# 24 columns a step on VectorE, loads of 16 and 8 registers, one-hot rows of two groups at once, 180 tiles copied

## The chip, the cores and the metric

The kernel runs on one core of a Trainium2 chip. The core has a matrix engine (PE, TensorE), a vector engine (DVE, VectorE), a scalar engine (ACT, ScalarE), GpSimd (POOL) and SyncE (SP), each with its own stream of instructions, and 16 DMA engines. The metric is the device time of one execution in microseconds (us), as a median over several runs. A profile of one execution gives the span of its instructions and the records that are quoted here.

## The reference

One layer of a graph network on 12,500 nodes of 64 numbers and 212,500 edges of 32, sorted by destination, with a residual and a layer norm:

```python
msg_in = concatenate([nodes[row], nodes[col], edge_features], axis=-1)
messages = relu(msg_in @ mW1 + mb1) @ mW2 + mb2
aggregated = segment_sum(messages, col, num_segments=12500)
update = relu(concatenate([nodes, aggregated]) @ uW1 + ub1) @ uW2 + ub2
x = layernorm(nodes + update)
```

`row` is an edge's source and `col` its destination.

## The kernel before

**Tiling.** The edges lie in order of destination. A tile is 128 edges, a group is three tiles (`TG` = 3, `GE` = 384 edges), and there are `G` = 554 groups. As the edges are sorted, the destinations of a group lie in a window of `W` = 32 nodes, whose first node is read on the chip.

**A step.** The main loop (L560) has one step k for each group. PE runs three parts of three groups, one behind another (L574): `turn(k)`, which transposes the group's gathered rows and its one-hot rows; `hidden(k - 2)`, the first matmul of the message network; and `sums(k - 4)`, which adds the hidden rows into the window by a matmul with the one-hot rows. ScalarE copies the transposed rows out of PSUM (L351) and applies the relu (L377). VectorE adds the sums into `agg` and the edge counts into a row of `xc` (L406, L407), at an address that is read into a register. PE starts a step when what it needs of the steps before is there: the gather, the one-hot rows, ScalarE's copies, and the PSUM tiles (two sets, `own.ps[g % 2]`).

**One-hot rows.** `onehot(g)` (L326) compares each edge's place in the window with 0 to 31 and writes 128 x 3 x 32 numbers next to the gathered rows, in the ring `own.s` of eight buffers (`RING`). It is issued at the end of step k for group k + 2 (L588).

**Two ways to the source nodes.** A group's source rows come by indirect DMA from GpSimd, one for each tile (L149), issued four groups ahead (`AHEAD`). A gather waits until the transposes of the group that had the buffer before are done. For some groups (`COPIED`, L81), the first tile is not gathered: its 128 columns are copied from `xc`, which holds all nodes' features transposed on the chip, straight to the place where the transposed rows would go. `fetch(k)` (L475) does this in each step from 18 on: VectorE copies `VCOLS` = (8, 12) columns and ScalarE `ACOLS` = (12, 8). Each count stands for one load of so many registers (L490) with the addresses of the source columns, and then so many copies of a column of 64 numbers (L503 on VectorE, L505 on ScalarE). With 40 columns a step, 164 tiles are copied, and 1497 are gathered.

**Every fourth step** has more: `places` reads four windows' addresses into registers (L301, a load of 4) and copies the four windows of `xc` (L308); `windows` multiplies them on PE (L315), and VectorE copies the four results to `wm` (L320). When 512 nodes have all their edges, an update of them is spread over three steps (`update`, L413: L424 to L458), 25 times in all. The indices of the next columns are scaled by VectorE every eighth step (L473).

**Order.** The order on each engine is that of the program. On VectorE a step is: the update's part if there is one, the two adds, the four copies to `wm` in every fourth step, the one-hot rows, the index scaling if due, a load of 8 and 8 copies, a load of 12 and 12 copies, and in every fourth step a load of 4 with four window copies.

Of the kernel before, what the change touches and what calls it, by code (L numbers as in the profile page):

```python
# [15 lines left out]
ALU = mybir.AluOpType  # L16
# [4 lines left out]
P = 128  # L21
N = 12500
E = 212500
D = 64
# [5 lines left out]
W = 32  # L30
TG = 3
GE = TG * P
G = (E + GE - 1) // GE
SB = 4
AHEAD = 4
RING = AHEAD + 4
BLOCKS = 3
NW = 2 * SB
NH = 3
# [7 lines left out]
TIMES = 4  # L47
BEGIN = 18
CHECKED = 8
VCOLS = (8, 12)  # L50
ACOLS = (12, 8)
COLS = sum(VCOLS + ACOLS)
SPAN = 8


def tiles_of(g):

    n = min(GE, E - g * GE)
    return [min(P, n - j * P) for j in range((n + P - 1) // P)]


def plan():
# [4 lines left out]
    def least(g):  # L67
        q = min(1.0, g * GE / E)
        return g * GE * N / E - 6.0 * math.sqrt((E - N) * q * (1 - q)) * N / E - 6

    chunks, b = [], 0
    for e in [c * CH for c in range(1, N // CH + 1)] + [N]:
        n = e - b
        chunks.append((b, *((P, n // P) if n % P == 0 else (n // 2, 2)),
                       next((g for g in range(G) if least(g) >= e), G)))
        b = e
# [4 lines left out]
COPIED = []  # L81
while BEGIN - (-P * (len(COPIED) + 1) // COLS) < G - SHORT:
    COPIED.append(BEGIN - (-P * (len(COPIED) + 1) // COLS))


class Own:
# [4 lines left out]
    def __init__(self, nc, ctx):  # L91
        def on(name, *shape, of=nc.sbuf_tensor):
            return ctx.enter_context(of(name, list(shape), F32)).ap()

        self.s = [on(f"own_s{i}", P, TG, D + W) for i in range(RING)]
        self.st = [on(f"own_st{i}", P, SB * GE) for i in range(BLOCKS)]
        self.wm = [on(f"own_wm{i}", P, H) for i in range(NW)]
        self.h = [on(f"own_h{i}", P, TG, H) for i in range(NH)]
        self.ident = on("own_ident", P, P)
        self.one = on("own_one", P, 1)  # L100
        self.at = (nc.sbuf_base + 31) // 32 * 32
        self.xc = on("own_xc", P, NP)

        self.ps = [[on(f"own_ps{i}{k}", P, 512, of=nc.psum_tensor) for k in range(3)]
                   for i in range(2)]
# [3 lines left out]
def ordered(ctx: ExitStack, tc: tile.TileContext, a, own, ok):  # L109
# [3 lines left out]
    nc = tc.nc  # L113
# [17 lines left out]
    loads, places_by, copy_by, relu_by, sums_by, wm_by, turn_by = ({} for _ in range(7))  # L131
# [3 lines left out]
    def after(first, *others):  # L135

        tc.declare_no_dep(first.ins, group="quiet", reason="waits for the last of a step")
        for i in others:
            tc.add_manual_dep(
                first.ins, i.ins.name,  # L140
                mybir.DependencyInfo(mybir.DependencyClass.Sync, mybir.DependencyReason.DATA),
                reason="the kernel's own rings",
            )
        return first
# [31 lines left out]
    iota = iop.tile([P, W], F32, name="iota")  # L176
# [3 lines left out]
    nc.vector.memset(xc[:, N:], 0.0)  # L180
    first_i = temp.tile([P, G], I32, name="first_i")
    nc.sync.dma_start(first_i, a["firsts"].to_broadcast([P, G]))
    dlc_i = temp.tile([P, G * TG], I32, name="dlc_i")
    nc.sync.dma_start(dlc_i, a["dst_cols"])
# [13 lines left out]
    def bit(k):  # L198

        nodes = [NEAR_NODES + (N - NEAR_NODES) * i // BITS for i in (k, k + 1)]  # L200
        tiles = [first + (NT - first) * i // BITS for i in (k, k + 1)]
        nc.sync.dma_start(src_sb[:, slice(*tiles)], a["src"][:, slice(*tiles)])
        nc.sync.dma_start(xc[:D, slice(*nodes)], a["xT"][:, slice(*nodes)])


    halves = [(0, G // 2), (G // 2, G)]
    firsts_f = [own.ps[0][k][:, : g1 - g0] for k, (g0, g1) in enumerate(halves)]
# [12 lines left out]
    dlc = const.tile([P, G * TG], F32, name="dlc")  # L220
# [30 lines left out]
    def combined():  # L251

        wps = ups.tile([H, CH], F32, name="u_ps").rearrange("p (n h) -> p n h", n=4)
        nc.tensor.matmul(wps[:, 0], w2t, u1s, start=True, stop=True)
        nc.tensor.matmul(wps[0:1, 1], b2, u1s, start=True, stop=True)
        nc.vector.tensor_copy(wc, wps[:, 0])
        nc.vector.tensor_copy(ux[D : D + 1, :], wps[0:1, 1])
# [27 lines left out]
    def inputs(b):  # L285
        if b * SB >= G:
            return
        c0, c1 = b * SB * GE, min(E, (b + 1) * SB * GE)
        efs_by[b] = nc.sync.dma_start(own.st[b % BLOCKS][D + W :, : c1 - c0], a["efT"][:, c0:c1])
        after(efs_by[b], *([hidden_by[(b - BLOCKS + 1) * SB - 1]] if b >= BLOCKS else []))  # L290

    def columns(g):
        t, c = own.st[g // SB % BLOCKS], (g % SB) * GE
        return t, c, sum(tiles_of(g))

    def places(b):

        g, n = b * SB, min(SB, G - b * SB)
        if n <= 0:
            return  # L300
        _, v = nc.values_load_multi_w_load_instructions(  # L301
            start_i[0:1, g : g + n], engines=[ET.DVE], min_val=0, max_val=N - 1,
            skip_runtime_bounds_check_because="they were clamped to the nodes on the chip",
        )
        xw = xwp.tile([D + 2, SB, W], F32, name="xw")
        for i in range(n):
            starts[g + i] = v[i]
            nc.vector.tensor_copy(xw[:, i, :], xc[:, bass.ds(v[i], W)])  # L308
        xws[b] = xw, n
# [16 lines left out]
    def onehot(g):  # L326
        if g >= G:
            return
        places_by[g] = nc.vector.tensor_tensor(  # L329
            own.s[g % RING][:, :, D:], iota.unsqueeze(1).to_broadcast([P, TG, W]),  # L330
            dlc[:, g * TG : (g + 1) * TG].unsqueeze(2).to_broadcast([P, TG, W]), ALU.is_equal,
        )
        after(places_by[g], *([sums_by[g - RING]] if g >= RING else []))

    def turn(g, ps):

# [132 lines left out]
    def addresses(i):  # L469

        if i in indices:
            t = indices[i][:, : min(SPAN * COLS, P * len(COPIED) - i * SPAN * COLS)]
            nc.vector.tensor_scalar(t, t, 4.0, float(own.at), ALU.mult, ALU.add)  # L473

    def fetch(k):  # L475
# [8 lines left out]
        c0 = (k - BEGIN) * COLS  # L484
        for engine, count in [*((ET.DVE, c) for c in VCOLS), *((ET.Activation, c) for c in ACOLS)]:
            count = min(count, P * len(COPIED) - c0)
# [37 lines left out]
    def step(*work):  # L524


        parts, used = [], []
        for part, g in work:
            ps, old = own.ps[g % 2], users[part][g % 2]
            parts.append((part, g, *part(g, ps)))  # L530
            used += old
        did = [i for p in parts for i in p[2]]
        after(did[0], *used, *(i for p in parts for i in p[3]))
        copies = None
        for part, g, *_ in parts:
            if part is sums:
                for b in [b for b in xws if (b - 1) * SB <= g][:1]:
                    last, copies = windows(b, own.ps[g % 2][2][:, (TIMES + 1) * W :][:, :H])
                    did.append(last)
        for i in did[:-1]:  # L540
            tc.no_tile_sem_insts.add(i.ins.name)
            tc.add_to_no_dep_group("quiet", i.ins)
        for part, g, _, _, follow in parts:
            if part is sums:
                step_update(g)
            users[part][g % 2] = follow(did[-1])
            if part is sums and copies:
                copies()
                users[part][g % 2] += [wm_by[b * SB + i] for i in range(min(SB, G - b * SB))]

    inputs(0)
    inputs(1)
    onehot(0)
    onehot(1)
    places(0)
    windows(0, ups.tile([H, CH], F32, name="u_ps")[:, :H], False)[1]()
    indexes(0)
# [2 lines left out]
    for k in range(G):  # L560
        if k < BITS:
            bit(k)
        if k == CHECKED:
            addresses(0)
            combined()
            ordered_edges()
            early.close()
            up = ctx.enter_context(tc.tile_pool(name="upd", bufs=2))
        if k % SB == 2:
            inputs(k // SB + 2)  # L570
        if k % SB == 1:
            places(k // SB + 1)
        if k < G - SHORT:
            step((turn, k), *([(hidden, k - 2)] if k > 1 else []),  # L574
                 *([(sums, k - 4)] if k > 3 else []))
            made, summed = max(0, k - 1), max(0, k - 3)
        else:

            step((turn, k))
            for _ in range(2):  # L580
                if summed < made:
                    step((sums, summed))
                    summed += 1
            for _ in range(2):
                if made <= k:
                    step((hidden, made))
                    made += 1
        onehot(k + 2)  # L588
        fetch(k)
        if k + AHEAD < G:  # L590
            gather(k + AHEAD)
# [333 lines left out]
```

## Time and profile before

| | us |
|---|---|
| median of 3 runs | 1896.92 |
| lowest and highest | 1896.71, 1897.36 |
| the profiled execution | 1895.77 |
| span of its instructions | 1894.0 |

| engine | busy us | share of the span |
|---|---|---|
| PE | 1362.3 | 72% |
| VectorE | 1490.7 | 79% |
| ScalarE | 1555.3 | 82% |
| GpSimd | 1417.9 | 75% |

The granted clock of TensorE was 0.969. In the profile's groups a line stands as: source line, engine, operation, what it writes and reads, how often; then busy time in us and the mean of one in ns; then the idle time of the engine just before these instructions, and what ended it. "issue" means that the profile shows nothing that the engine waited for. DVEq and ACTq are the engines' instruction streams: loads of registers stand there and are not counted as busy. In a timeline a line has its start and length in us, and merged instructions carry a count.

### The profile page before, as it was taken

How to read it: one execution, taken by the hardware profiler on the slowest of the kernel's cores; microseconds unless marked ns; L12 is line 12 of the kernel's file. 1: busy time of each engine (PE TensorE's matmuls, PEld its weight loads, DVE VectorE, ACT ScalarE, POOL GpSimd, SP SyncE). 2: the span in 40 equal slices, each digit the busy share in tenths (PEclk: the TensorE clock that was granted, in tenths of full speed). 3: DMA queues.
4: the chain of work that ended last, by engine and by line, in shares of the span. 5: the costliest groups of instructions: out<-in, count | busy, mean ns of one | idle time of the engine just before them, and what ended most of it. 6: DMA issues, size and time to landing. Idle time of an engine off the chain costs nothing. (4 is left out here: it accounts for less than half of the span.)

```text
span 1894.0 us, 58313 instructions
## 1 busy us (share of the span) xinstructions
PE 1362.3 (72%) x12209; PEld 1194.1 (63%) x12209; DVE 1490.7 (79%) x13761; ACT 1555.3 (82%) x11818; POOL 1417.9 (75%) x1504
## 2 busy tenths in 40 slices
PE   3776777767767777677776776876767778767777
PEld 3666666666666666666665665766656667666665
DVE  3578888778888788887888878888888888887883
ACT  3489889888898888887988888889888888898882
POOL 7777777777777777777777777777777777777774
PEclk9999999999999999999999999999999999999999
DMA  5322222222222222222222222222222222222221
GB/s 136 73 46 45 46 48 44 51 44 47 46 45 48 46 43 51 45 47 43 48 51 43 48 46 45 46 48 44 51 44 48 46 47 45 47 44 50 47 44 29
DMA packets 68443, 92.52 MB, mean 49 GB/s; under 512 B 30893, under 2 KB 38350, under 8 KB 68078
## 3 DMA queue, kind: packets, MB, share of 16 engines
q0 software_dynamic: 47904, 49.12, 14.7%
q1 hardware_dynamic: 19260, 39.12, 7.2%
q14 instruction: 263, 2.15, 0.4%
q8 instruction: 102, 1.67, 0.4%
q10 hardware_dynamic: 914, 0.46, 0.1%
HBM read 85.29 MB, written 3.20 MB: 47 GB/s over the span
## 5 line engine op out<-in xcount | busy, mean ns | idle before, releaser
L149 POOL DMA_INDIRECT own_s<-in_x,src_sb x1497 | 1417.1, 947 | 457.4 <-issue 336.2
L503 DVE COPY own_st<-own_xc 64x4 uint8 x10500 | 895.3, 189 | 233.9 <-issue 221.5
L505 ACT ACTIVATE own_st<-own_xc 64x4 uint8 x10492 | 1058.0, 194 | 18.5 <-issue 15.4
L341 PE MATMUL own_ps<-own_ident,own_s 128*96 128x128 f32 x1661 | 289.1, 285 | 497.5 <-DMA own_s<-in_x,src_sb 149.2
L341 PEld LDWEIGHTS own_ps<-own_ident,own_s 128*96 128x96 f32 x1661 | 169.0, 132 | 567.8 <-ACT own_h L377 261.3
L394 PE MATMUL own_ps<-own_s,own_h 128*128 128x128 f32 x3322 | 481.3, 283 | 3.5 <-ACT own_h L377 3.0
L366 PE MATMUL own_ps<-own_wm,own_st 128*128 128x128 f32 x3322 | 478.8, 282 | 0.0
L351 ACT ACTIVATE own_st<-own_ps 96x384 f32<-96x384 f32 (+2 forms) x718 | 294.0, 410 | 203.8 <-PE own_ps L399 105.3
L394 PEld LDWEIGHTS own_ps<-own_s,own_h 128*128 128x128 f32 x3322 | 434.0, 199 | 5.1 <-ACT own_h L377 4.1
L366 PEld LDWEIGHTS own_ps<-own_wm,own_st 128*128 128x128 f32 x3322 | 431.0, 198 | 1.4 <-issue 0.5
L377 ACT ACTIVATE own_h<-own_ps 128x384 f32<-128x384 f32 x553 | 264.0, 477 | 15.0 <-PE own_ps L366 15.0
L399 PE MATMUL own_ps<-own_s,own_one 128*1 128x32 f32 x3322 | 190.2, 194 | 0.0
L320 DVE COPY own_wm<-own_ps 32x128 f32<-32x128 f32 x550 | 156.9, 285 | 5.6
L399 PEld LDWEIGHTS own_ps<-own_s,own_one 128*1 128x1 f32 x3322 | 114.6, 84 | 69.8 <-issue 6.7
L406 DVE TENSOR_TENSOR agg<-own_ps,agg 128x32 f32 x554 | 105.5, 190 | 64.3 <-PE own_ps L399 27.7
L329 DVE TENSOR_TENSOR own_s<-iota,dlc 128x96 f32<-128x96 f32 x554 | 142.5, 258 | 14.3 <-issue 0.2
L407 DVE TENSOR_TENSOR own_xc<-own_ps,own_xc 1x32 f32 x554 | 101.1, 183 | 29.3 <-PE u_ps L425 10.1
L308 DVE COPY xw<-own_xc 66x32 f32 x554 | 72.5, 214 | 15.3 <-DMA own_xc<-in_xT 9.2
L315 PE MATMUL own_ps<-w1b,xw 66*128 66x128 f32 (+1 forms) x276 | 69.1, 333 | 0.0
L446 ACT ACTIVATE rstd<-mv,eps 128x4 f32<-128x4 f32 (+1 forms) x25 | 7.4, 297 | 55.7 <-DVE mv L444 55.7
L437 PE MATMUL u_ps<-u,u 128*128 128x64 f32 (+1 forms) x196 | 50.3, 400 | 0.5 <-ACT u L427 0.5
L437 PEld LDWEIGHTS u_ps<-u,u 128*128 128x128 f32 (+1 forms) x196 | 47.2, 325 | 2.2 <-ACT u L427 0.9
(62 smaller groups left out, 278.0 us busy)
## 6 DMA issues: line engine op xcount, KB each, us to landing
own_st<-in_efT SPq DMA_DIRECT2D x138, 192.0 KB
own_s<-in_x,src_sb POOLq DMA_INDIRECT x1497
xin<-in_x SPq DMA_DIRECT2D x24, 128.0 KB
out<-o SPq DMA_DIRECT2D x24, 128.0 KB
own_xc<-in_xT SPq DMA_DIRECT2D x12, 179.2 KB
index<-in_src_copied SPq DMA_DIRECT2D x65, 1.2 KB
dlc_i<-in_dst_cols SPq DMA_DIRECT2D x1, 831.0 KB
own_xc<-in_xT SPq DMA_DIRECT2D x4, 179.5 KB
```

The costliest lines, as they stand in the source:

```text
L149: nc.gpsimd.indirect_dma_start(out=s[:p, j, :D], out_offset=None, in_=x[:, :], in_offset=bass.IndirectOffsetOnAxis(ap=src_sb[:p, g * TG + ...
L320: c = nc.vector.tensor_copy(wm[g % NW][D : D + W, :], wp[i * W : (i + 1) * W, :])
L329: places_by[g] = nc.vector.tensor_tensor(own.s[g % RING][:, :, D:], iota.unsqueeze(1).to_broadcast([P, TG, W]), dlc[:, g * TG : (g + 1) * ...
L341: nc.tensor.transpose(xt[:, j * P : j * P + p], s[:p, j, :], ident[:p, :p])
L351: after(nc.scalar.activation(t[r, c : c + n][:, m], xt[r, m], AF.Copy), step)
L366: nc.tensor.matmul(pre[:p, j, :], t[:, c + j * P : c + j * P + p], wm[g % NW], start=True, stop=True)
L377: relu_by[g] = [nc.scalar.activation(h, pre, AF.Relu)]
L394: did.append(nc.tensor.matmul(sg, h[:p, j, :], s[:p, j, D:].unsqueeze(1).to_broadcast([p, TIMES, W]), start=j == 0, stop=j == len(sizes) - 1))
L399: did.append(nc.tensor.matmul(counted, own.one[:p], s[:p, j, D:], start=j == 0, stop=j == len(sizes) - 1))
L406: after(nc.vector.tensor_tensor(agg[:, at], sg[:, 0, :], agg[:, at], ALU.add), step),
L503: by[engine] = nc.vector.tensor_copy(o, x_at)
L505: by[engine] = nc.scalar.activation(o, x_at, AF.Copy)
```

## The change

Three things are changed. VectorE copies 24 columns a step in place of 20, after a load of 16 registers and then one of 8, in place of 8 and then 12. The number of columns a step becomes 44, so that the formula at L81 gives 180 copied tiles in place of 164. The one-hot rows of two groups are written by one operation, issued in even steps alone, for which the ring's buffers are made in pairs. ScalarE's columns stay at 20 a step.

```diff
-VCOLS = (8, 12)
+VCOLS = (16, 8)
 ACOLS = (12, 8)
...
-        self.s = [on(f"own_s{i}", P, TG, D + W) for i in range(RING)]
+        self.two = [on(f"own_s{i}", P, 2 * TG, D + W) for i in range(RING // 2)]
+        self.s = [t[:, h * TG : (h + 1) * TG] for t in self.two for h in (0, 1)]
...
-        places_by[g] = nc.vector.tensor_tensor(
-            own.s[g % RING][:, :, D:], iota.unsqueeze(1).to_broadcast([P, TG, W]),
-            dlc[:, g * TG : (g + 1) * TG].unsqueeze(2).to_broadcast([P, TG, W]), ALU.is_equal,
+        places_by[g] = places_by[g + 1] = nc.vector.tensor_tensor(
+            own.two[g % RING // 2][:, :, D:], iota.unsqueeze(1).to_broadcast([P, 2 * TG, W]),
+            dlc[:, g * TG : (g + 2) * TG].unsqueeze(2).to_broadcast([P, 2 * TG, W]),
+            ALU.is_equal,
         )
-        after(places_by[g], *([sums_by[g - RING]] if g >= RING else []))
+        after(places_by[g], *([sums_by[g + h - RING] for h in (0, 1)] if g >= RING else []))
...
     onehot(0)
-    onehot(1)
...
-        onehot(k + 2)
+        if k % 2 == 0:
+            onehot(k + 2)
```

A group of 128 columns now ends every 2.9 steps in place of every 3.2, and the columns change hands between VectorE and ScalarE at other places.

More of the change, by code (lines that the diff above doesn't have):

```diff
@@ L33 @@
 G = (E + GE - 1) // GE
+assert G % 2 == 0
 SB = 4
```

## The prediction

> **What bounds the kernel now.** I read the busy totals first, then the idle columns of the costliest groups, then the timeline of one engine at a time.
>
> ```profile
> L149 POOL DMA_INDIRECT own_s<-in_x,src_sb x1497 | 1417.1, 947 | 457.4 <-issue 336.2
> L503 DVE COPY own_st<-own_xc 64x4 uint8 x10500 | 895.3, 189 | 233.9 <-issue 221.5
> ...
> 200.00:1800.00 1600.00, 1162.23 (x10490) 1020.37 (x10490) 1308.63 (x12276) 1374.44 (x10664) 1210.11 (x1280) 0.97 0.22 46
> ```
>
> The last line gives PE, weight loads, VectorE, ScalarE and GpSimd in turn. GpSimd looks only 75% busy, but 1280 gathers in 1600 us are one every 1.250 us, and the longest idle time before a gather in the table of waits is 1.4 us, once (0.3 otherwise): 0.947 of work and 0.30 of issue, without a pause. So the 1497 gathers make 1497 x 1.250 = 1871 us of the 1894, and 23 us lie at the ends. A step with copied columns (there are 525) issues 3 x 525 - 164 = 1411 gathers, 1764 us: 3.36 us a step. That is the bound. VectorE's column copies have 221.5 us of idle time that nothing explains but "issue". What that is shows in VectorE's own timeline, with the registers' loads beside it:
>
> ```profile
> 1006.55 0.19 DVE L406 TENSOR_TENSOR agg<-own_ps,agg 128x32 f32 x1
> ...
> 1009.50 0.17 DVE L406 TENSOR_TENSOR agg<-own_ps,agg 128x32 f32 x1
> 1009.70 0.18 DVE L407 TENSOR_TENSOR own_xc<-own_ps,own_xc 1x32 f32 x1
> 1009.92 0.26 DVE L329 TENSOR_TENSOR own_s<-iota,dlc 128x96 f32<-128x96 f32 x1
> 1010.44 0.67 DVE L503 COPY own_st<-own_xc 64x4 uint8 x8 [0.27 <-issue]
> 1011.61 1.21 DVE L503 COPY own_st<-own_xc 64x4 uint8 x12 [0.50 <-issue]
> 1012.49 0.33 DVE L406 TENSOR_TENSOR agg<-own_ps,agg 128x32 f32 x1
> ...
> 1015.13 0.20 DVE L406 TENSOR_TENSOR agg<-own_ps,agg 128x32 f32 x1
> ...
> 1019.03 0.19 DVE L406 TENSOR_TENSOR agg<-own_ps,agg 128x32 f32 x1
> ```
>
> ```profile
> L490 DVEq TENSOR_LOAD <-index x10: 593/720/845, 1004.2 to 1019.3; - x10
> ...
> L301 DVEq TENSOR_LOAD <-start_i x139: 339/344/596, 11.8 to 1863.6; - x139
> ```
>
> The second fence is the view of one source line: least, median and longest duration in ns. Ten loads at L490 split into those of 8 registers (0.595) and of 12 (0.845); L301 loads 4 (0.344). That is 62.6 ns a register and 94 ns besides. The engine's instruction stream hands nothing on while it loads, so the engine drains what it holds and then stands: the 0.27 and 0.50 us above. In the single records a step's stream is a strict chain: load of 8 (0.595), 0.322 to hand over 8 copies, load of 12 (0.845), 0.45 for 12 copies, 0.42 for the adds' register operations and the one-hot: 2.63, which is the step from 1012.49 to 1015.13 (2.64). A copy costs the engine 0.071 us (8 starts in a row), but the stream only (0.45 - 0.322)/4 = 0.032. The other ordinary steps (2.95, 2.99) hold a further pause of some 0.35 us, about once in four steps. The fourth, 1015.13 to 1019.03, has the four window copies (L320) and the next window reads (L308), whose 1.18 us of engine work cover both loads: 3.90. Four steps: 12.48, or 3.12 a step. All 525 average 3.36, so 0.24 a step (126 us) is the node updates and VectorE's waits for others; the waits are 94 us of it (the rows of agg, y and own_xc, from 27.7 down to 10.1). VectorE thus keeps up with GpSimd by a small margin only, though the page says 79% busy.
>
> **The change part by part.** Sums are against the profiled span of 1894.0 us; the runs' median, 1896.92, is 2.9 above it.
>
> *Gathers.* 180 tiles copied in place of 164 remove 16 gathers: 16 x 1.250 = 20 us off GpSimd's chain, giving 1874. Per column step GpSimd then needs (3 x 525 - 180) x 1.250 / 525 = 3.32 us. Whatever else takes over 3.32 a step decides.
>
> *Loads of 16 and 8.* No row has a load of 16. By the line through 4, 8 and 12 it is 94 + 16 x 62.6 = 1.095 us; below it can't sensibly be under the 12's 0.845, above two loads of 8 (1.19) bound it. I take 1.095. With 0.595 for the 8 that is 1.69 a step against 1.44: +0.25.
>
> One page speaks strongly against loading more registers. The Trainium skill, Runtime: NRT & Kernel Launch, Instruction fetch mechanics, puts a TENSOR_LOAD at about 200 ns a register; by it four more would cost 0.8 us a step and the sum would be some 420 us longer. The rows here show 62.6 ns, and 20 registers at 200 ns would not have fitted in the 3.36 us step of today.
>
> *Four more copies.* In the stream 4 x 0.032 = +0.13; on the engine 4 x 0.071 = +0.28, where the engine is the limit.
>
> *One-hot of two groups.* One operation in place of two takes about 0.03 from the stream every second step: -0.02. On the engine it is 128x192, which the trace does not have. Between 0.26 (as now) and 0.52 (twice) I take 0.36: from 32 elements at 0.190 (L406) to 96 at 0.258 an element costs 1.06 ns. It falls on the window steps (each has one), so there +0.10; the step without one loses 0.26 us of cover under the load of 16. It waits for the sums of two groups, the later one five steps back, long done.
>
> *An ordinary step* is bound by the stream: +0.25 + 0.13 - 0.02 = +0.36, so 3.00 plus pauses. Nothing covers it: a load of 1.095 has at most the add of own_xc and the one-hot (0.2 to 0.6 us) before it, so VectorE stands 0.5 to 0.9 us ahead of each 16 copies. Three of them: +1.08. From agg to agg 0.19 comes off once in four steps: the engine ends a step trailing its stream by the last copies, and 8 leave a lag of 0.33 where 12 left 0.52.
>
> *A window step* is bound by the engine: +0.28 (copies) +0.10 (one-hot) +0.18 (the load of 4 for L308 now stands behind 8 copies, 0.57 us, and no longer hides) -0.16 (the gap between the two groups of copies goes): +0.40.
>
> *Sum.* Four steps: 12.48 + 1.08 - 0.19 + 0.40 = 13.77, 3.44 a step, already over GpSimd's 3.32. The updates' own share stays (126 - 94 = 32 us, 0.06 a step; most of their 88 us of VectorE work lies in load gaps). Of the 94 us of waits, 0.18 a step, I keep 0.04: when VectorE is last, PE's results mostly lie ready; the bounds are 0 and 0.18. So 3.54 a step. 525 x (3.54 - 3.36) = +95 us: a span of 1989, with 2.9 around it **1992**.
>
> What is late next: PE's transposes (L341) need the one-hot and the PSUM that the adds (L406, L407) free, so PE, then ScalarE, then the freeing of own_s by the transposes are all paced by VectorE, and GpSimd starts to pause. ScalarE's 20 columns are as they were; the 16 split copies of L351 add some 0.18 us each, off the path.
>
> **The rivals.**
>
> A. *VectorE stays within GpSimd's pace*, so that the gain stands: 1874 + 3 = 1877, faster. It needs a step under 3.32, that is, 0.22 less than my sum. For it: a load of 16 at 0.845 (-0.25 in three of four steps, -0.19) and no waits (-0.04) would just do. Against it: three sizes of load lie on one line, and the chain 2.63 matches a measured step to 0.01.
>
> B. *The load gaps keep their size* and only engine work counts: the 16 copies cover the load of 8, which pays for the longer first load. Then a step is 2.75 busy (1308.63 x 3.36/1600), +0.28 copies, -0.08 one-hots, +0.42 gaps (221.5/525) = 3.37: 525 x 0.01 = 5 us, 1902. For it: window steps do hide loads. Against it: in the ordinary steps the stream, not the engine, sets 2.64.
>
> C. *VectorE's waits do not shrink*: all 0.18 remains, as updates are a round trip over PE and ScalarE (the sqrt of L446 waits 55.7 us for VectorE). 3.44 + 0.06 + 0.18 = 3.68: +168, 2065.
>
> **How the numbers follow.** Forecast 0.70, A 0.07, B 0.10, C 0.13. About 0.2% is what this kernel's measurement can tell from no change (1893 to 1901). Faster: A and a little of B, 0.09; same: part of B, 0.04; slower 0.87. Around the forecast the unknowns are the load (-99 to +37 us over 525 steps, three of four), the wide one-hot (-13 to +21, one in four) and the waits (-21 to +74). The range runs from 1922, short of B, to 2075, over C: A and B, 0.17, lie outside it.
>
> **What would show it.** Right: 1481 gathers at the same 947 ns but spaced wider than 1.25 us, with idle time now put down to PE or the transposes; VectorE's loads at L490 (L493 in the new file) near 595 and 1095 ns in equal numbers; "issue" idle before its copies up from 221.5 to about 300 us; agg to agg near 3.0 in ordinary and 4.3 in window steps; PE waiting for VectorE's lines. Wrong: gathers still every 1.25 us (A or B), a load of 16 well under 1.0 us, or VectorE's waits for PE still near 94 us with a step of 3.6 or more (C).

## The result, and the profile after

The changed kernel takes 2012.89 us (median of 5 runs, 2011.43 to 2014.55); the kernel before took 1896.92 in runs beside it (1896.71 to 1897.70). The ratio is 1.0609, 95% interval 1.0597 to 1.0621: 116 us slower, where 95 us were forecast. The profiled execution has a span of 2012.2 us against 1894.0, that is, 118.2 us more.

The costliest groups of the changed kernel (line numbers are two or three higher than before: L151 is the gather, L506 VectorE's column copy, L409 and L410 the adds, L344 the transposes, L331 the one-hot rows):

```profile
L151 POOL DMA_INDIRECT own_s<-in_x,src_sb x1481 | 1401.2, 946 | 572.2 <-issue 384.0
L506 DVE COPY own_st<-own_xc 64x4 uint8 x12576 | 999.9, 188 | 304.1 <-issue 283.6
...
L344 PE MATMUL own_ps<-own_ident,own_s 128*96 128x128 f32 x1661 | 302.7, 295 | 544.2 <-ACT own_st L508 191.1
...
L331 DVE TENSOR_TENSOR own_s<-iota,dlc 128x192 f32<-128x192 f32 x277 | 99.1, 358 | 6.0
```

The longest of VectorE's waits for PE (in all in us, then the number of waits and the longest, as the view has them):

```profile
DVE agg L409 <- PE own_ps L402: 24.5, 13, 4.7
DVE agg L409 <- PE own_ps L317: 13.3, 7, 3.1
DVE y L442 <- PE u_ps L440: 11.4, 11, 3.8
```

There are 16 gathers fewer, each as long as before, but their idle time grew from 457 to 572 us. In the timeline GpSimd keeps its 1.25 us for some stretches and then stops; in the rows below, 4.02 us pass from one start to the next. From 200 to 1800 us it issues 1194 gathers where it had issued 1280 (in the second fence, the windows' line of that stretch, the count behind the last busy time):

```profile
1030.54 0.94 POOL L151 DMA_INDIRECT own_s<-in_x,src_sb  x1 [0.30 <-issue]
1031.79 0.94 POOL L151 DMA_INDIRECT own_s<-in_x,src_sb  x1 [0.30 <-issue]
1035.81 0.94 POOL L151 DMA_INDIRECT own_s<-in_x,src_sb  x1 [3.08 <-PE own_ps L317]
```

```profile
200.00:1800.00 1600.00, 1136.42 (x9811) 999.79 (x9811) 1301.03 (x13059) 1280.07 (x9998) 1128.06 (x1194) 0.94 0.20 43
```

So GpSimd is no longer the bound: it waits for PE to have read the ring. In the table of waits (in all in us, number, longest) its two rows for PE have 168 us and up to 4.1 at a time; in the kernel before, the larger row for PE (second fence) had none over 0.3:

```profile
POOL own_s L151 <- PE own_ps L402: 116.4, 124, 3.8
POOL own_s L151 <- PE own_ps L317: 51.7, 42, 4.1
```

```profile
POOL own_s L149 <- PE own_ps L399: 28.6, 94, 0.3
```

VectorE's own timeline shows what has taken its place:

```profile
1000.73 0.18 DVE L409 TENSOR_TENSOR agg<-own_ps,agg 128x32 f32 x1
1000.94 0.18 DVE L410 TENSOR_TENSOR own_xc<-own_ps,own_xc 1x32 f32 x1
1001.16 0.36 DVE L331 TENSOR_TENSOR own_s<-iota,dlc 128x192 f32<-128x192 f32 x1
1002.03 1.26 DVE L506 COPY own_st<-own_xc 64x4 uint8 x16 [0.52 <-issue]
1003.54 0.66 DVE L506 COPY own_st<-own_xc 64x4 uint8 x8 [0.25 <-issue]
1004.12 0.17 DVE L409 TENSOR_TENSOR agg<-own_ps,agg 128x32 f32 x1
1004.32 0.18 DVE L410 TENSOR_TENSOR own_xc<-own_ps,own_xc 1x32 f32 x1
1005.36 1.89 DVE L506 COPY own_st<-own_xc 64x4 uint8 x24 [0.85 <-issue]
1007.16 0.17 DVE L409 TENSOR_TENSOR agg<-own_ps,agg 128x32 f32 x1
```

VectorE stands still during the load of 16: 0.52 us here in the step with a one-hot operation, 0.85 in the step without one. Over all ordinary steps in the records (those without window copies or an update) it is 0.44 us on average with one, and 0.81 to 0.95 without. The two steps take 3.39 and 3.04 us. The load of 8 costs 0.25 in the first and nothing in the second.

PE follows VectorE, although the table of waits does not say so. It puts 191.1 us of the transposes' waiting down to ScalarE's column copies and 106.8 to "issue", and next to nothing to VectorE. The single records tell more: of the 317 times that PE stood for over 0.5 us before a transpose, 303 ended 0.08 to 0.15 us after the end of a VectorE add (L410) or one-hot (L331). In the kernel before it was 164 of 373. PE's wait is for several semaphores, and the view names one of them only; the times of the starts point to VectorE as the last.

### The profile page after: what moved, and what is told of

It reads as the page before. It is cut to its first block, busy times and chain, and to the rows that moved or that the text cites. A ratio compares the mean times of both kernels' runs of the same rounds, so it can differ in the third digit from the quotient of the medians.

```text
span 2012.2 us, 60054 instructions
## 1 busy us (share of the span) xinstructions
PE 1425.1 (71%) x12209; PEld 1251.8 (62%) x12209; DVE 1576.8 (78%) x15560; ACT 1543.6 (77%) x11806; POOL 1402.0 (70%) x1488
## 5 line engine op out<-in xcount | busy, mean ns | idle before, releaser
L151 POOL DMA_INDIRECT own_s<-in_x,src_sb x1481 | 1401.2, 946 | 572.2 <-issue 384.0
L506 DVE COPY own_st<-own_xc 64x4 uint8 x12576 | 999.9, 188 | 304.1 <-issue 283.6
L344 PE MATMUL own_ps<-own_ident,own_s 128*96 128x128 f32 x1661 | 302.7, 295 | 544.2 <-ACT own_st L508 191.1
L344 PEld LDWEIGHTS own_ps<-own_ident,own_s 128*96 128x96 f32 x1661 | 174.8, 136 | 614.4 <-ACT own_st L508 206.9
L397 PE MATMUL own_ps<-own_s,own_h 128*128 128x128 f32 x3322 | 503.6, 292 | 4.1 <-ACT own_h L380 3.6
L369 PE MATMUL own_ps<-own_wm,own_st 128*128 128x128 f32 x3322 | 505.2, 293 | 0.0
L397 PEld LDWEIGHTS own_ps<-own_s,own_h 128*128 128x128 f32 x3322 | 456.4, 208 | 6.2 <-ACT own_h L380 5.2
L369 PEld LDWEIGHTS own_ps<-own_wm,own_st 128*128 128x128 f32 x3322 | 458.0, 209 | 1.8 <-issue 0.5
L402 PE MATMUL own_ps<-own_s,own_one 128*1 128x32 f32 x3322 | 192.4, 196 | 0.0
L402 PEld LDWEIGHTS own_ps<-own_s,own_one 128*1 128x1 f32 x3322 | 116.1, 84 | 72.3 <-issue 12.4
L409 DVE TENSOR_TENSOR agg<-own_ps,agg 128x32 f32 x554 | 105.9, 191 | 43.3 <-PE own_ps L402 24.5
L410 DVE TENSOR_TENSOR own_xc<-own_ps,own_xc 1x32 f32 x554 | 101.1, 183 | 20.4 <-DVE agg L409 1.4
L331 DVE TENSOR_TENSOR own_s<-iota,dlc 128x192 f32<-128x192 f32 x277 | 99.1, 358 | 6.0
L310 DVE COPY xw<-own_xc 66x32 f32 x554 | 77.7, 211 | 25.2 <-DMA own_xc<-in_xT 9.4
```

Source lines behind the costliest of these rows:

```text
L151: nc.gpsimd.indirect_dma_start(out=s[:p, j, :D], out_offset=None, in_=x[:, :], in_offset=bass.IndirectOffsetOnAxis(ap=src_sb[:p, g * TG + ...
L344: nc.tensor.transpose(xt[:, j * P : j * P + p], s[:p, j, :], ident[:p, :p])
L369: nc.tensor.matmul(pre[:p, j, :], t[:, c + j * P : c + j * P + p], wm[g % NW], start=True, stop=True)
L397: did.append(nc.tensor.matmul(sg, h[:p, j, :], s[:p, j, D:].unsqueeze(1).to_broadcast([p, TIMES, W]), start=j == 0, stop=j == len(sizes) - 1))
L402: did.append(nc.tensor.matmul(counted, own.one[:p], s[:p, j, D:], start=j == 0, stop=j == len(sizes) - 1))
L409: after(nc.vector.tensor_tensor(agg[:, at], sg[:, 0, :], agg[:, at], ALU.add), step),
```

## The experiments

Four theories stand against each other. **S**: VectorE's instruction stream, register loads plus the handing over of copies, became longer than GpSimd's gathers. **E**: the engine time of four more copies costs it. **O**: the paired one-hot rows cost it. **W**: the waits between VectorE's and ScalarE's columns cost it. Each kernel is compared with the kernel before on the same chip.

| run | median us | before | ratio, 95% interval |
|---|---|---|---|
| e1_onehot_alone | 1896.78 | 1897.01 | 0.9998, 0.9989 to 1.0008 |
| e2_columns_alone | 2008.72 | 1897.01 | 1.0588, 1.0571 to 1.0606 |
| e3_one_load_of_8 | 1876.50 | 1897.01 | 0.9891, 0.9875 to 0.9908 |
| e4_longer_loads | 1958.51 | 1897.01 | 1.0326, 1.0304 to 1.0348 |
| e5_load_of_24 | 2458.75 | 2391.69 | 1.0283, 1.0239 to 1.0326 |
| e6_8_then_16 | 2410.90 | 2391.69 | 1.0105, 1.0047 to 1.0162 |
| e8_20_and_22 | 3042.26 | 2391.69 | 1.2709, 1.2653 to 1.2766 |
| e9_22_and_22 | 3163.05 | 2391.69 | 1.3230, 1.3173 to 1.3286 |
| e5b_load_of_24 | 2084.11 | 1897.49 | 1.0991, 1.0973 to 1.1009 |
| e11_44_in_turns | 1953.33 | 1897.49 | 1.0300, 1.0282 to 1.0317 |
| e12_scalar_22_in_turns | 1887.38 | 1896.65 | 0.9949, 0.9936 to 0.9963 |
| e13_scalar_24 | 1878.30 | 1896.65 | 0.9902, 0.9887 to 0.9917 |

**The two parts apart.** First the one-hot rows alone, then the columns alone:

```diff
--- after.py
+++ e1_onehot_alone
-VCOLS = (16, 8)
+VCOLS = (8, 12)
--- before.py
+++ e2_columns_alone
-VCOLS = (8, 12)
+VCOLS = (16, 8)
```

> The paired one-hot rows alone: columns and loads as before (8 then 12, 40 a step, 1497 gathers). Theory S (VectorE's instruction stream, which is the sum of register loads and hand-overs, became longer than GpSimd's gathers): the stream loses 0.02 us a step, the window step's engine work grows by 0.10, and GpSimd's 1497 gathers of 1.25 us still decide: 1897, within 6 us. Rival O (the paired one-hot costs the time, as one operation of 192 elements that also waits for two groups' sums): a good part of the 116 us shows here, over 1920.

> The columns alone: 24 behind loads of 16 and 8, 180 tiles copied, one-hot rows group by group as before. S: nearly the changed kernel, 2005 to 2025 (0.02 us a step more in the stream, 0.10 less in every fourth step on the engine). O: most of the loss is gone, under 1950.

Measured: no change, and 2008.7. The one-hot rows cost nothing, and the columns alone have nearly all of the loss (112 of 116 us). O falls.

**The same copies with fewer registers.** The changed kernel keeps its 24 copies, but they take their addresses from one load of 8:

```diff
--- after.py
+++ e3_one_load_of_8
-            _, v = nc.values_load_multi_w_load_instructions(
-                indices[i][0:1, b : b + count], engines=[engine],
...
-            for q, at in zip(range(c0, c0 + count), v):
+            if engine == ET.DVE and count == VCOLS[1] and c0 > (k - BEGIN) * COLS:
+                v = again
+            else:
+                _, v = nc.values_load_multi_w_load_instructions(
+                    indices[i][0:1, b : b + min(count, 8 if engine == ET.DVE else count)],
+                    engines=[engine],
...
+                again = v
+            for q, at in zip(range(c0, c0 + count), [*v, *v]):
```

> The changed kernel with all its 24 copies, waits and 1481 gathers, but VectorE loads 8 registers a step in place of 16 and 8, and uses the 8 addresses three times, so that 16 of VectorE's 24 columns hold other nodes' features than they should. S: the stream falls to 0.42 + 0.60 + 0.83 = 1.85 us in an ordinary step, less than the engine's 2.3, and both lie under GpSimd's 3.32, so the gathers decide again: 1877, within 8 us. Rival E (the engine time of four more copies, 0.28 us a step) and rival W (the semaphore waits between VectorE's and ScalarE's columns, more of them with 44 columns than with 40) have lost nothing: 2013.

Measured: 1876.5. VectorE's timeline of this kernel:

```profile
1001.10 0.17 DVE L409 TENSOR_TENSOR agg<-own_ps,agg 128x32 f32 x1
1001.31 0.18 DVE L410 TENSOR_TENSOR own_xc<-own_ps,own_xc 1x32 f32 x1
1001.52 1.88 DVE L511 COPY own_st<-own_xc 64x4 uint8 x24
1003.32 0.17 DVE L409 TENSOR_TENSOR agg<-own_ps,agg 128x32 f32 x1
```

All 24 copies run without a pause, and the step shown is 2.22 us; the mean of 2.74 in the table further down holds waits, as GpSimd decides again. It is back at 1280 gathers in the same 1600 us:

```profile
200.00:1800.00 1600.00, 1174.81 (x10596) 1033.04 (x10595) 1363.09 (x14071) 1382.70 (x10781) 1210.25 (x1280) 0.97 0.21 47
```

PE's long pauses end right behind a VectorE add or one-hot only 91 times of 329 here. E and W fall together: the number of copies, their waits and the gathers are those of the changed kernel, and 136 us are gone with 16 registers a step.

**The same registers with fewer copies.** The kernel before, in which VectorE's load of 8 becomes one of 12 while the copies stay 8 and 12:

```diff
--- before.py
+++ e4_longer_loads
-                indices[i][0:1, b : b + count], engines=[engine],
+                indices[i][0:1, b : b + (12 if engine == ET.DVE else count)], engines=[engine],
```

> The kernel before with its 20 copies, 164 tiles and 1497 gathers, but VectorE's load of 8 is a load of 12 of which 8 registers are used, so that it loads 24 registers a step (94 + 750 ns twice = 1.69 us, as the changed kernel does). S: ordinary steps 0.25 us longer, window steps nearly not, 0.19 a step on VectorE's 3.12, plus updates and waits of 0.15 as in the changed kernel: 3.46 against 3.36, 1950 (1935 to 1965). E and W: nothing is added on the engine or between the engines, 1897.

Measured: 1958.5. Four unused registers a step cost 61 us in a kernel that copies nothing more. Together with e3 this shows S, from both sides.

**The loads in other shapes.** These four ran on another chip, on which the kernel before took 2391.7 us:

```diff
--- after.py
+++ e5_load_of_24
-VCOLS = (16, 8)
+VCOLS = (24,)
+++ e6_8_then_16
+VCOLS = (8, 16)
+++ e8_20_and_22
+VCOLS = (20,)
-ACOLS = (12, 8)
+ACOLS = (12, 10)
+++ e9_22_and_22
+VCOLS = (22,)
-ACOLS = (12, 8)
+ACOLS = (12, 10)
```

> The changed kernel with one load of 24 registers ahead of the 24 copies on VectorE. S: the load is 94 + 24 x 62.6 = 1.60 us in place of 1.69 for the two, one hand-over less by 0.07, but the engine's queue now holds back the end of the hand-over: ordinary steps about 0.08 shorter, and in window steps the load of 4 hides again behind the long run of copies (0.18): some 55 us less than the changed kernel's 2013, 1955 (1940 to 1980). E: the same copies, 2013.

> The changed kernel with the load of 8 first and the load of 16 second. S: the same registers and hand-overs in a step, so the ordinary step's stream is as long; the 16 copies at a step's end leave the engine a longer queue, so the load of 4 in the window step hides (0.18) and the lag on entering it is longer (0.2): 0.3 to 0.4 less in four steps, 40 to 50 us less than 2013, 1968 (1955 to 1995). E: 2013.

> Paired one-hot rows, VectorE's 20 columns behind one load of 20 (1.35 us in place of 1.44), ScalarE 22 behind 12 and 10: 42 columns, 172 tiles, 1489 gathers. S: VectorE's stream is shorter than before, GpSimd decides: 1897 - 8 x 1.25 = 1887 (1882 to 1892), if ScalarE's two more copies (0.19 us a step on some 2.95) find room. Rival: ScalarE is then last and the time is 1897 or more.

> Paired one-hot rows, VectorE 22 columns behind one load of 22 (94 + 22 x 62.6 = 1.47 us, about the 1.44 of before), ScalarE 22 behind 12 and 10: the 44 columns, 180 tiles and 1481 gathers of the changed kernel. S: VectorE's step is 0.0 to 0.1 longer than before (3.2 to 3.3 with updates) and just under GpSimd's 3.32: 1877 to 1890. E: 22 copies are half of the way to 24, 1940 or more.

Measured: ratios of 1.03, 1.01, 1.27 and 1.32 to a kernel that was itself 26% slower there; all four expectations missed. Their times tell nothing of the step's sum; e6, the other order of the two loads, stays open, as it was not run on another chip. But the loads' own durations are the usual ones where the counts are usual (596 and 1097 ns in e6), and in e8 and e9 they are not. The view of the loads' line, least, median and longest in ns, in e8, e9 and then in e5b (below):

```profile
L493 DVEq TENSOR_LOAD <-index x525: 603/1605/4744, 120.0 to 2986.8; - x175
```

```profile
L493 ACTq TENSOR_LOAD <-index x1047: 1346/2202/2871, 117.7 to 3092.8; - x175
L493 DVEq TENSOR_LOAD <-index x524: 1814/1819/2073, 118.0 to 3087.2; - x175
```

```profile
L493 DVEq TENSOR_LOAD <-index x524: 1596/1602/1870, 79.1 to 2021.3; - x175
```

24 registers take 1.60 us, on the line through 4, 8, 12 and 16. But 22 take 1.81, where the line has 1.47. In e8, with 42 columns a step, every second load begins 8 bytes past a multiple of 16 bytes, counted from the start of the index buffer: those loads of 20 take 4.45 to 4.74 us (262 of them), the aligned ones 1.35 (256 records, most of the rest). ScalarE's loads of 12 go from 0.78 to 2.55 in the same way. So both kernels carried a cost that no theory had, and E was not tested by them.

**One load of 24 again, and 44 columns by turns.**

```diff
--- after.py
+++ e11_44_in_turns
-VCOLS = (16, 8)
-ACOLS = (12, 8)
+VCOLS = ((24,), (20,))
+ACOLS = ((12, 8), (12, 12))
...
-        for engine, count in [*((ET.DVE, c) for c in VCOLS), *((ET.Activation, c) for c in ACOLS)]:
+        for engine, count in [*((ET.DVE, c) for c in VCOLS[odd]),
+                              *((ET.Activation, c) for c in ACOLS[odd])]:
```

> The kernel of e5_load_of_24 once more, as there the kernel before took 2392 us on the same chip, 26% more than on the others, and nothing can be told from that. S as there: 1955 (1940 to 1980) where the kernel before takes 1897. E: 2013.

> Paired one-hot rows, and 44 columns in every step with all loads at multiples of four registers: in even steps VectorE 24 behind one load (1.60 us) and ScalarE 8 and 12, in odd steps VectorE 20 behind one load (94 + 20 x 62.6 = 1.35 us) and ScalarE 12 and 12. 180 tiles and 1481 gathers, as in the changed kernel. S: four steps of VectorE are 2.5 + 2.9 + 2.5 + 4.25 and a pause of 0.35, 3.13 a step, with updates and waits 3.30, about GpSimd's 3.32: 1877 to 1892, 10 us or more under the kernel before. E: VectorE copies 22 on average, half of the added engine time stays: over 1940. Rival: ScalarE, with 22 in place of 20, is last: over 1900.

Measured: 2084.1 and 1953.3; both expectations missed, by 104 us or more and by 61. One load in place of two makes the kernel 71 us slower than the changed kernel, not 55 faster (on another chip, but the kernel before differs by only 0.6 us between the two). VectorE's timeline of e5b:

```profile
1003.71 0.26 DVE L409 TENSOR_TENSOR agg<-own_ps,agg 128x32 f32 x1
...
1005.12 1.86 DVE L506 COPY own_st<-own_xc 64x4 uint8 x24 [0.91 <-issue]
1006.90 0.17 DVE L409 TENSOR_TENSOR agg<-own_ps,agg 128x32 f32 x1
...
1010.88 0.17 DVE L409 TENSOR_TENSOR agg<-own_ps,agg 128x32 f32 x1
...
1012.72 1.88 DVE L506 COPY own_st<-own_xc 64x4 uint8 x24 [1.46 <-issue]
1014.52 0.17 DVE L409 TENSOR_TENSOR agg<-own_ps,agg 128x32 f32 x1
```

The steps are 3.19 and 3.64 us, where 2.9 was expected. In the records the stream comes to the next step's first register operation 1.13 us after the load of 24 ends (median of 368 steps); 24 copies at 0.032 would have taken 0.83. At that time 14 copies have started and ten wait. After a load of 16 the stream hands on all 16 copies in 0.56 us, with nine waiting at its end. So the stream gets only some ten copies ahead of the engine; the end of a longer run goes at the engine's 0.071 us a copy, and the register operations of the adds come behind it. With 16 copies and then a load of 8, the load runs while the engine still has copies; with one long run it cannot. The Trainium skill, Advanced Engine Details and Errata, Engine Queue Depths, gives VectorE a queue of 8. The trace agrees roughly, with nine or ten copies waiting. My sum for one load had allowed for the queue at the copies but not at the adds. With it the stream is 0.42 + 1.60 + 1.13 = 3.15 us, and the second and third ordinary steps after a window step average 3.18 and 3.14. The first one takes 3.62; that further pause is not explained.

By its number alone e11's 1953 would also suit E (over 1940) and a ScalarE that is last (over 1900). Other runs speak against both: e3 has 24 copies on VectorE in every step and loses nothing, and e13 below has 24 on ScalarE in every step and is faster than the kernel before. In e11's records 278 of PE's 291 long pauses end right behind a VectorE add or one-hot, and the ordinary steps with 24 columns behind one load take 3.22 us, those with 20 take 2.60 and, right after a window step, 3.08. The sum had 2.9 and 2.5.

**The added columns on ScalarE.** VectorE keeps 8 and 12:

```diff
--- e11_44_in_turns
+++ e12_scalar_22_in_turns
-VCOLS = ((24,), (20,))
-ACOLS = ((12, 8), (12, 12))
+VCOLS = ((8, 12), (8, 12))
+ACOLS = ((12, 12), (12, 8))
--- after.py
+++ e13_scalar_24
-VCOLS = (16, 8)
-ACOLS = (12, 8)
+VCOLS = (8, 12)
+ACOLS = (12, 12)
```

> Paired one-hot rows, VectorE as before (8 and 12 columns), the added columns on ScalarE: 12 and 12 in even steps, 12 and 8 in odd ones, every load a multiple of four registers from a multiple of four. 42 columns a step, 172 tiles, 1489 gathers. S: VectorE's stream is that of the paired one-hot rows alone (1897 with 1497 gathers) and GpSimd decides: 8 x 1.25 = 10 us less, 1887 (1883 to 1892). Rival: VectorE or ScalarE has no room left at 3.34 us a step, 1897 or more.

> Paired one-hot rows, VectorE as before (8 and 12), ScalarE 24 behind 12 and 12 in every step: the 44 columns, 180 tiles and 1481 gathers of the changed kernel, with the four added columns on ScalarE. S: if both engines fit under GpSimd's 3.32 us a step, 1877. ScalarE's busy time is 2.89 us a step in the kernel before (1374.44 us in 1600 us); four copies of 0.095 and the split copies make it 3.29, so that any wait of its own makes it the last: 1885 to 1910 is likelier, still some 100 us under the changed kernel. E (added copies as such cost the time) does not tell the engines apart and has 1990 or more.

Measured: 1887.4 and 1878.3, both a little faster than the kernel before (0.5% and 1.0%, with intervals that lie clear of 1). The engines and the gathers of e13:

```profile
PE 1365.7 (73%) x12209; PEld 1198.4 (64%) x12209; DVE 1445.6 (77%) x13464; ACT 1711.1 (91%) x13902; POOL 1403.3 (75%) x1488
```

```profile
L151 POOL DMA_INDIRECT own_s<-in_x,src_sb x1481 | 1402.5, 947 | 452.6 <-issue 329.4
```

e13 has the 180 copied tiles and 1481 gathers of the changed kernel, and GpSimd decides again: 18.4 us less than before, near 16 x 1.25 = 20. ScalarE had the room that VectorE lacked. I had thought it likelier that ScalarE would be last, at 1885 or more; instead its waits shrank (it waits 24 us for the sums, PE's L402, where it had waited 105).

## Why the prediction was right

The times from agg to agg in the single records, in us, are means over the 515 steps from the 20th sum on. The first two columns are steps without an update: ordinary ones, and those with window copies. The third is what the mean of all steps (the last column) has above three ordinary steps and one window step:

| kernel | ordinary | window | updates and waits | all |
|---|---|---|---|---|
| before | 2.88 | 3.92 | 0.23 | 3.37 |
| changed | 3.11 | 4.41 | 0.15 | 3.59 |
| e4_longer_loads | 3.09 | 4.04 | 0.16 | 3.48 |
| e3_one_load_of_8 | 2.74 | 4.11 | 0.25 | 3.33 |
| e5b_load_of_24 | 3.31 | 4.30 | 0.16 | 3.71 |

*The bound before* was GpSimd, with VectorE close under it: e12 and e13 took 8 and 16 gathers away, left VectorE's loads and copies alone, and gained 9.3 and 18.4 us, which is 1.16 and 1.15 us a gather, somewhat under the 1.25 of its pace.

*The load of 16* was 1.095 us in the forecast and is 1.097 to 1.10 in the records. The 200 ns a register of the Trainium skill, Runtime: NRT & Kernel Launch, Instruction fetch mechanics, would make it 3.2; that page speaks of registers loaded from HBM at a launch, and these loads read an index buffer in SBUF. For loads that are aligned and a multiple of four registers the trace does not bear 200 ns out, but the unaligned ones of e8 come near it: 4.45 us for 20 is 0.22 each.

*Four steps* came to 13.77 us in the forecast, 3.44 a step; three ordinary steps and one window step of the table, before rounding, are 13.75. That they agree to 0.02 is partly luck, as three terms were off and cancel. The four steps taken as the basis (12.48) are 0.08 shorter than the mean. The ordinary steps grew by 0.23 us each, not by the 0.30 that +1.08 and -0.19 make for three. The window step grew by 0.49 and not by 0.40. The arithmetic of the stream itself holds: the third ordinary step after a window step has a median of 2.64 us before, as the chain has it, and 3.03 after, with +0.36 forecast. What the sum did not have is that the further pauses got shorter. The forecast calls them once in four steps, although two of the three ordinary steps it shows have one; it kept them as they stand there, and they shrank on average from 0.24 to some 0.11 us an ordinary step.

e4 confirms the loads' term by itself, in the sum: 0.25 us more of loading in three steps of four is 0.19, and its steps without updates are 0.19 longer (3.14 to 3.33). It is spread otherwise than expected: 0.21 in ordinary steps, and 0.12 in window steps, which were to hide it.

*The one-hot rows* were 0.36 us on the engine as estimated (358 ns), and hidden altogether in the kernel before (e1).

*What was mis-sized in the end* is the waits kept: 0.04 us a step of the 0.18. VectorE's rows of waits for PE sum to 53 us after (24.5, 13.3, 11.4, 2.9 and 0.7), 0.10 a step. The rest of the table's 0.15, 0.05, is near the 0.06 put for the updates' own share. So a step is 3.59 and not 3.54, and 525 x 0.05 = 26 us covers the 23 us between the span of 1989 forecast and the 2012.2 measured. So rival C had a part of the truth: the waits went down to a little over half.

*What would show it*: 1481 gathers with pauses ended by PE, loads of 595 and 1097 ns, and 283.6 us of "issue" (some 300 foreseen) came as written; the steps, 3.11 and 4.41 where 3.0 and 4.3 were named, came near it. That PE would be seen waiting for VectorE did not: the table names ScalarE, and only the times of the starts show VectorE.

*Rivals* A and B are out: e3 shows that A is what happens when the loads are short. B let the gaps keep their size, and the "issue" time before the copies rose from 221.5 to 283.6 us, with 0.44 to 0.95 us ahead of the 16 copies.

## What to carry to other kernels

Look at an engine's instruction stream as well as at its busy time: VectorE was 79% busy and had hardly any room, as 1.44 us of each 3.37 us step went into register loads, during which nothing new reached the engine. Before giving an engine more work to relieve another, add up its stream for one step, loads and hand-overs, and look for an engine that has room (here ScalarE, whose copies had only 15 us of "issue" time ahead of them). Idle time of some 0.2 us or more put down to "issue" ahead of short operations was the sign here, and an experiment that changes the loads but not the work settles it in one run.

## What the runs showed of the hardware

- On VectorE a load of n registers took 94 + 62.6 n ns for n = 4, 8, 12, 16, 20 and 24 (344 ns to 1602), if it started at a multiple of 16 bytes in the index buffer. ScalarE's load of 12 took 0.78 us. Loads that started 8 bytes past such a place took some 0.21 us a register (12 in 2.55 us on ScalarE, 20 in 4.45 on VectorE), and 22 from an aligned start took 1.81.
- VectorE's stream hands a copy on in 0.032 us, the engine takes 0.071, and the stream gets some ten copies ahead (e5b: 14 of 24 started when the last has been handed on).
- The granted clock of TensorE was lower in the kernels that VectorE paced: 0.969 before and in e3 and 0.964 in e13, but 0.944 in e4, 0.933 in the changed kernel and 0.922 in e5b. PE was not the bound there (it stood idle for 544 us before the transposes of the changed kernel), and why the clock falls is not shown.
- One chip ran the kernel before in 2391.7 us. Single operations there were as long as elsewhere (948 ns a gather in e5, as in e5b), but waits appeared that the others lack: own_xc (L410) waited 156.4 us for the add just before it in e5, against 0.3 us in e5b, the same kernel on another chip. The cause stays open.
